# A two-direction state-space layer with its feed-forward part: B·C and the state update placed between the two parts of the outputs in twelve chunk pairs

## The chip, the core and the metric

The kernel runs on one core of a Trainium2 chip. The core has TensorE (matmuls, PE; its weight loads are listed apart as PEld), VectorE (DVE), ScalarE (ACT), GpSimd (POOL) and SyncE (SP), which here only issues DMAs. Each engine works through its own instructions in their order and waits on semaphores for the others. Matmuls write to PSUM, eight banks that TensorE, VectorE and ScalarE share; everything else lies in SBUF. The metric is the device time of one execution in microseconds (us); less is better.

## What is computed

Eight sequences of 512 tokens with 256 features pass through a layer norm, a state-space block (Mamba-2) once forward and once on the reversed sequence, a projection of both results with a residual, a second layer norm, and a feed-forward part with a low-rank correction, again with a residual. All of it is in 32-bit floats. The reference of one direction, cut:

```python
zxbcdt = x @ Win
z, xBC, dt = jnp.split(zxbcdt, [D_INNER, D_INNER + CONV_CH], axis=-1)
xBC = _silu(conv(xBC, convw) + convb)            # 4 taps along the sequence
xs, Bm, Cm = jnp.split(xBC, [D_INNER, D_INNER + NGROUPS * D_STATE], axis=-1)
dt = softplus(dt + dtb)
dA = exp(dt * -exp(Alog))
h = dA_t * h + dt_t * B_t * x_t                  # per head, 64 states, step by step
y_t = C_t . h
y = (y + D * xs) * silu(z)
y = y * rsqrt(mean(y * y) + 1e-05) * normw
return y @ Wout
```

There are 512 inner channels in 8 heads of 64, and 64 states.

## The kernel before

**Tiling.** A sequence is cut into four chunks of 128 tokens. A *pair* (b, c) is chunk c of the forward direction of sequence b together with chunk 3-c of the backward one; the 32 pairs are worked off in order (b, c). Within a chunk the recurrence is written as matrix products: the outputs of a pair are the sum of what the state at the chunk's start gives (h with C, scaled by the decay) and what the chunk's own tokens give (x times dt, with a 128x128 matrix per head, `lam`, which holds decays times B·C).

**The main loop** (`for i in range(n)`, L964) handles in iteration i the pair p = i and prepares the pair q = i+1, and mixes in pieces of other work: blocks of the input projection and convolution of the next sequences (`Block.project`, `tap`, `convolve`, `silu`; the blocks of an iteration are called `work[0]` to `work[3]`), gate projections (`Gates.project`, tile pz), and the tails of finished chunks (`Tail`: output projection pm, second norm, feed-forward pf, store). The order of instructions on each engine is the order in which the loop writes them; `pin()` (L60) fixes it at the end of each iteration. No scheduler moves anything.

**The steps of a pair on TensorE, by line.** `outputs` (L637): the state's part, from h and dec, for chunks 1 to 3 (32 matmul instructions; each 32-bit matmul is two instructions, a transpose one), and then the part within the chunk, from xdt and lam (32); both add into the two tiles py (L643). `add_state` (L657): pst (L663), the chunk's contribution to the state. `turn` (L584): transposes of q's x, tiles pxs (L588). `work[0].project`: pp (L419). `Tail.turn`: pxt (L784). `norm_sum`: ss (L702). A gate: pz (L499). `cb` (L603): B·C of q (L609), from which `mix` (L614) makes q's lam. Then pf (L791), pm (L751), and the other blocks and gates.

**The steps on the other engines.** VectorE: `evict` (L675) adds py into yg; `new_state` (L665) adds pst to the decayed state in chunks 1 and 2 (in chunk 0 it is a copy, on ScalarE); `scan` (L570) and `mix` make lam; `convolve` (L432) takes three instructions per block; the tail's `residual` (L758) and `add_ffn` (L794) read pm and pf. ScalarE: `tap` (L430), copies of the turned tiles (L590, L786), silus, squares (L691), the sums for the norm (L709), `skip` (L623). GpSimd: `times_gate` (L684), `scale_x` (L599), `scale_c` (L566), `decay_state` (L633), and small norm arithmetic. In each odd sequence, chunks 1 and 2 also hold the series that turns the raw step sizes of the next two sequences into dt and decays (`Steps`, L326, on ScalarE and VectorE).

**PSUM.** One bank holds a constant; the other seven are pools, in each of which tiles take turns: p_proj with 3 banks (pp, pz, pst), p_tr with 2 (pxs, pxt, ss, cb and other turned tiles), p_y with 2 (py, pf, pm). A tile waits until the last reader of the tile that had its bank before is done. The pools are set up as follows:

```python
p_proj = ctx.enter_context(tc.tile_pool(name="p_proj", bufs=3, space=PSUM))
p_tr = ctx.enter_context(tc.tile_pool(name="p_tr", bufs=2, space=PSUM))
p_y = ctx.enter_context(tc.tile_pool(name="p_y", bufs=2, space=PSUM))
```

Of the kernel before, what the change touches and what calls it, by code (L numbers as in the profile page):

```python
# [14 lines left out]
P = 128  # L15
NB, L, DM = 8, 512, 256
NC = L // P
DI = 512
NS = 64
NH, HD = 8, 64  # L20
NK = DM // P
NBLK = DI // P
# [9 lines left out]
def tile_bimamba_ffn(  # L32
# [39 lines left out]
    pe, dve, act, pool, sp = nc.tensor, nc.vector, nc.scalar, nc.gpsimd, nc.sync  # L72
# [4 lines left out]
# [3 lines that stand above are left out]
# [8 lines left out]
    def ps(p, shape, name):  # L88
        return p.tile(shape, F32, name=name, tag=p.name)
# [32 lines left out]
    for d in range(2):  # L122
# [4 lines left out]
        rows = slice(d * 64, (d + 1) * 64)  # L127
# [150 lines left out]
    def softplus_v(b0, of):  # L278
        v, e = sm("v", b0) if b0 == 0 else of, sm("e", b0)
        act.activation(v, of, AF.Identity, bias=dtb_col[:, 0:1])  # L280
        act.activation(e, v, AF.Abs)
        act.activation(e, e, AF.Exp, scale=-1.0)
        return v, e

    def steps_raw(b0):

        half = L // 2
        pd = ps(p_tr, [P, half], f"pdt_{b0}")
        quarters = [(i, j) for i in range(NSG) for j in range(2)]
        for k in range(NK):  # L290
            for n, (i, j) in enumerate(quarters):
                pe.matmul(
                    pd[32 * n:32 * (n + 1), :], lhsT=wd2[:, k, :],
                    rhs=seq[b0 + i]["xhT"][:, k, j * half:(j + 1) * half],
                    start=(k == 0), stop=(k == NK - 1), skip_group_check=True, tile_position=(0, 32 * n),
                )
        raw = convp.tile([P, half], F32, name=f"raw_{b0}", tag="raw", bufs=1)
        act.copy(raw, pd)
        return b0, raw
# [82 lines left out]
    def steps_last(b0):  # L382
        g = seq[b0]["g"]
        last = g["last"] = sm("last", b0, (P, 64))
        act.activation(last[F], fold[F], AF.Copy, scale=upto[F, P:])
        act.activation(last[W], fold[W], AF.Copy, scale=onward[W, 0:1])

    def steps_by_token(b0):
        g = seq[b0]["g"]
        dt, wl = g.pop("rows")  # L390
        pt = ps(p_tr, [P, 2, P], f"pdw_{b0}")
        pe.transpose(pt[:, 0, :], dt, ident)
        pe.transpose(pt[:, 1, :], wl, ident)
        g["dw"] = sm("dw", b0, (P, 2, P), bufs=2)
        act.copy(g["dw"], pt)
# [128 lines left out]
    class Pair:  # L524
# [58 lines left out]

        def turn(m, d, pool_of=None):  # L584

            pt = ps(pool_of or p_tr, [P, DI], f"pxs_{m.name}_{d}")
            for blk in range(NBLK):
                pe.transpose(pt[:, blk * P:(blk + 1) * P], m.s["xc", d][:, blk, m.tcol[d]], ident)  # L588
            m.xw[d] = m.tile("xs", (P, DI), 4, d)
            act.copy(m.xw[d], pt)  # L590
# [43 lines left out]
                    hb(m.h_new), hb(m.s["h"]), tot.unsqueeze(2).to_broadcast([P, NH, HD]), ALU.mult  # L634
                )

        def outputs(m):  # L637

            m.py = [ps(p_y, [P, NBLK, P], f"py_{m.name}_{d}") for d in range(2)]

            def add(d, h, lhsT, rhs, first, last):
                blk, two = divmod(h, 2)
                pe.matmul(  # L643
                    m.py[d][two * HD:(two + 1) * HD, blk, :], lhsT=lhsT, rhs=rhs, start=first, stop=last,
                    skip_group_check=True,
                )

            order = [(d, 2 * blk + two) for blk in range(NBLK) for d in range(2) for two in range(2)]
            if m.c:
                for d, h in order:  # L650
                    rows = slice(d * NS, (d + 1) * NS)
                    add(d, h, m.s["h"][rows, h * HD:(h + 1) * HD], m.dec[rows, h, :], h < 2, False)
            for d in range(2):
                for h in range(NH):
                    add(d, h, m.xdt[d][:, h * HD:(h + 1) * HD], m.lam[d][:, h, :], m.c == 0 and h < 2, h >= NH - 2)

        def add_state(m):  # L657
            if m.c == NC - 1:
# [36 lines left out]
        def squares(m):  # L695
            return m.s["gates", m.c // 2].sz[:, :, :, m.c % 2, :]

        def norm_sum(m):

            m.ss = ps(p_proj if (m.b, m.c) == (NB - 1, 1) else p_tr, [P, 2, P], f"ss_{m.name}")  # L700
            for d in range(1 if m.folded else 2):
                pe.transpose(m.ss[:, d, :], m.squares()[:, d, 0, :], ident)  # L702

# [21 lines left out]
    class Tail:  # L725
# [51 lines left out]
        def bias2(t):  # L777
            t.adds.tensor_tensor(t.x1[:, 0, :], t.x1[:, 0, :], bf_sb, ALU.add)

        def turn(t):  # L780
            at = begin[ends.index((t.b, t.c))]
            pt = ps(p_proj if at == n - 3 else p_tr, [P, NK, P], f"pxt_{t.name}")
            for k in range(NK):
                pe.transpose(pt[:, k, :], t.xh[:, k * P:(k + 1) * P], ident)  # L784
            t.xT = outp.tile([P, NK, P], F32, name=f"xT_{t.name}", tag="xT")
            act.copy(t.xT, pt)  # L786
# [14 lines left out]
    first = {key: Block(0, *key) for key in blocks}  # L801
# [9 lines left out]
    for half, (mv, rs) in enumerate(halves):  # L811
        for j in range(2):
            c = 2 * half + j
            dve.tensor_scalar(xh[:, c, :], xh[:, c, :], mv[:, j, 0:1], rs[:, j:j + 1], ALU.subtract, ALU.mult)
    seq[0]["xhT"] = seqp.tile([P, NK, L], F32, name="xhT_0", tag="xhT", bufs=3)
    pt = [ps(p_tr, [P, L], f"pxh_0_{k}") for k in range(NK)]
# [14 lines left out]
    def conv(*key):  # L831
        first[key].convolve()
# [27 lines left out]
    st = Steps(0, *softplus_v(0, pdt))  # L860
# [12 lines left out]
    order = [(b, c) for b in range(NB) for c in range(NC)]  # L873
    n = len(order)
# [4 lines left out]
    q = pairs[0]  # L879
# [13 lines left out]
    gates.project_one(0, 0)  # L893
    gates.project_one(1, 0)
    steps_by_token(0)
    q.turn(0)
    conv(1, 2)
    q.scale_x(0)
    first[1, NBLK].silu()
# [34 lines left out]
    ends = [(b, c) for b in range(NB) for c in (1, 2, 0, 3)]  # L934

    begin = [min(j + NC - 1, n - 1 + (j % NC) // 2) if j >= n - NC else j + NC - 1 for j in range(n)]
    tails = {}

    def when(t, *what):
        for one in t if isinstance(t, list) else [t]:  # L940
            if one is not None:
                for w in what:
                    if w:
                        getattr(one, w)()

    def begun(at):
        return [tails[j] for j in range(n) if begin[j] == at]

    def gated(i):
# [10 lines left out]
            ones += [(g.project, g.silu, d, half) for half in range(2)]  # L960
        return ones

    st = raw = late = before = None
    for i in range(n):  # L964
        p, q = pairs[i], pairs.get(i + 1)
        b, c = order[i]
        t, t0 = begun(i), begun(i - 1)
        gates = None

        def gate(j):  # L970
            nonlocal gates
            if gates is None:
                gates = gated(i)
            if j < len(gates):
                gates[j][0](*gates[j][2:])

        def gate_silu(j):
            if j < len(gates):
                gates[j][1](*gates[j][2:])
# [3 lines left out]
        even = b % NSG == 0  # L983
# [10 lines left out]
        hold = q is not None and c == NC - 1  # L994
        if work[0] is None or hold:
            when(t0, "norm2")
        if b:
            p.decay_state()
            if q:
                q.scale_c()  # L1000
        p.outputs()

        soon = b and c < 2
        if soon:
# [4 lines left out]
        early = q is not None and b == NB - 1  # L1009
        if early:  # L1010
            q.scan(0)
        for d in range(2):
            p.evict(d)
            p.times_gate(d)
        p.add_state()
        p.new_state()
        if q:
            q.turn(0)
            if not hold:
                q.turn(1)  # L1020
        if hold:
            when(before, "norm_sum", "norm_mean")
            when(late, "silu")
        elif work[0] is not None:
            when(t0, "norm2")
# [4 lines left out]
        if hold:  # L1030
            if work[0] is None:
                gate(0)
            q.turn(1)
        if not q:
            when(t[:1], "bias1", "project")
        when(t0, "turn")
        if not hold:
            when(before, "norm_sum", "norm_mean")
        if not p.folded:
            for d in range(2):  # L1040
                p.square(d)
# [6 lines left out]
        if q:  # L1048
            if not hold or work[0] is not None:
                gate(0)  # L1050
            q.cb()
            gate_silu(0)
            if i == 0:
                steps_last(0)
            if p.folded:
                for d in range(2):
                    p.square(d)
            for d in range(2):
                q.scale_x(d)
# [50 lines left out]
        if raw is not None and c == 1:  # L1110
            st = Steps(b + 1, *softplus_v(b + 1, raw))
# [29 lines left out]
            q.decay_state()  # L1141
        when(work[2], "convolve")
        when(work[3], "convolve_aside")
        if st and not even and c == 2:
            steps_by_token(ahead)
            st = None
        late, before = work[2:] if i else work[1:], p
# [7 lines left out]
        if even and c == 3 and ahead < NB:  # L1155
            raw = steps_raw(ahead)
# [2 lines left out]


    t, t0 = begun(n), begun(n - 1)
    when(before, "norm_sum", "norm_mean")
    when(t0[:1], "scales", "norm2")
    when(t, "bias1")
    when(before, "norm_power")
    when(t0[:1], "bias2")
    when(t0[1:], "scales", "norm2")
    when(t, "project")
    when(t0, "turn")
    when(t[0], "residual")  # L1170
    when(t0[1:], "bias2")
    t[1].residual((0,))
# [3 lines left out]
    when(t0[:1], "add_ffn", "store")  # L1176
    when(t[1], "norm2_v")
    when(t0[1:], "add_ffn", "store")
    when(t, "bias2", "turn")
    for one in t:  # L1180
        when(one, "ffn", "add_ffn", "store")
    pin()
# [40 lines left out]
```

## Time and profile before

| what | value |
|---|---|
| median of three executions | 612.42 us (611.91 to 612.53) |
| the profiled execution | 612.31 us, span of its instructions 610.5 us |
| granted TensorE clock | 0.998 of full speed |
| VectorE busy in 180:220, 300:340, 340:380 (us of 40) | 39.09, 38.97, 38.01 |
| TensorE busy in the same | 40.00, 39.86, 40.00 |
| pp matmuls (L419) | 151.1 us, 320 instructions |
| pm (L751), pz (L499) | 115.8 us and 106.5 us |
| py (L643) | 63.0 us, 1024 instructions |
| py's weight loads | 55.3 us |

The profile is of one execution. A group's line gives engine, line, operation, tiles written and read, the sizes, the count and the times; of a matmul the part of the array in use stands first (128*128 is all of it, 64*64 a quarter). The ends of matmuls are modelled, so that the start of one group to the start of the next tells more than a duration. The chain of waits follows the work that ended last back in time; its shares tell which engine set the end where.

### The profile page before, as it was taken

What the parts mean: (1) busy time and instruction counts of PE and PEld (TensorE: products, weight loads), DVE (VectorE), ACT (ScalarE), POOL (GpSimd) and SP (SyncE); (2) the same over time, 40 slices, a digit from 0 to 9 for tenths busy, and PEclk for the clock granted to TensorE, in tenths of its full rate; (3) what the DMA queues carried; (4) which work ended last, traced back from release to release, by engine and by line L of the source; (5) the groups of instructions that cost most, each with busy time, mean ns of one, the idle gap of its engine ahead of it and who ended that gap; (6) DMA issues with size and microseconds to landing.
All of it is one profiled execution on the core that took longest, in us unless ns stands there. A gap on an engine that the chain in (4) does not pass through costs nothing.

```text
span 610.5 us, 11975 instructions
## 1 busy us (share of the span) xinstructions
PE 591.1 (97%) x4296; PEld 424.6 (70%) x4296; DVE 543.2 (89%) x818; ACT 437.9 (72%) x988; POOL 471.1 (77%) x580
## 2 busy tenths in 40 slices
PE   5989989999999999999999999999999999999997
PEld 2467757667776687766767677767767767777875
DVE  5888988889999989988999998988999998897964
ACT  3788796777877687885887877786978856755541
POOL 3287885787858898878859799678976889599983
PEclk9999999999999999999999999999999999999999
DMA  7476342123065323135025422443006442444011
GB/s 220 139 245 190 113 112 77 29 74 103 4 200 155 122 87 110 54 84 157 19 90 186 124 77 88 122 123 119 24 5 195 121 122 88 122 121 122 18 53 36
DMA packets 36252, 64.82 MB, mean 106 GB/s; under 512 B 8608, under 2 KB 23392, under 8 KB 36192
## 3 DMA queue, kind: packets, MB, share of 16 engines
q1 hardware_dynamic: 34048, 64.00, 34.7%
q8 instruction: 34, 0.56, 0.4%
q10 hardware_dynamic: 2144, 0.04, 0.2%
q14 instruction: 26, 0.21, 0.1%
HBM read 59.12 MB, written 4.72 MB: 105 GB/s over the span
## 4 chain that ended last, share of the span: by engine, by line
PE 67%; DVE 15%; ACT 10%; POOL 4%; issue 2%; DMA 1%; SPq 0%; DVEq 0%; ACTq 0%; POOLq 0%
PE pp L419 16%; PE pm L751 14%; PE pz L499 12%; PE py L643 10%; PE pf L791 4%; PE pxs L588 4%; DVE lam L577 4%; DVE xc L437 3%; PE pst L663 3%; PE cb L609 1%; DVE lam L615 1%; ACT yg L623 1%; ACT sz L691 1%; DVE yg L677 1%; ACT xc L455 1%
## 5 line engine op out<-in xcount | busy, mean ns | idle before, releaser
L437 DVE SCALAR_TENSOR_TENSOR xc<-pp,conv_sb,xc 128x511 f32<-128x511 f32 x180 | 133.4, 744 | 24.1 <-ACT xc L430 19.9
L419 PE MATMUL pp<-xhT,win_sb 128*128 128x512 f32 x320 | 151.1, 598 | 1.0 <-ACT v L280 0.5
L577 DVE TENSOR_TENSOR_SCAN lam<-lam,seed 128x512 f32<-128x512 f32 x128 | 145.7, 1198 | 0.5 <-DMA lam<-dat 0.5
L684 POOL TENSOR_TENSOR yg<-yg,sz 128x512 f32<-128x512 f32 x64 | 81.1, 1289 | 62.8 <-DVE yg L677 58.2
L751 PE MATMUL pm<-wy,yg 128*128 128x256 f32 x512 | 115.8, 379 | 0.0
L499 PE MATMUL pz<-xhT,win_sb 128*128 128x256 f32 x448 | 106.5, 380 | 0.3 <-ACT sz L522 0.3
L751 PEld LDWEIGHTS pm<-wy,yg 128*128 128x128 f32 x512 | 97.0, 190 | 13.4 <-issue 0.3
L499 PEld LDWEIGHTS pz<-xhT,win_sb 128*128 128x128 f32 x448 | 82.4, 190 | 17.7 <-issue 5.3
L419 PEld LDWEIGHTS pp<-xhT,win_sb 128*128 128x128 f32 x320 | 57.8, 192 | 46.8 <-issue 42.0
L623 ACT ACTIVATE yg<-xc,dcol 128x128 f32<-128x128 f32 x256 | 81.3, 393 | 0.5
L615 DVE TENSOR_TENSOR lam<-lam,cb 128x1024 f32<-128x1024 f32 x64 | 74.9, 1211 | 0.5 <-PE cb L609 0.5
L430 ACT ACTIVATE xc<-pp,conv_sb 128x512 f32<-128x512 f32 x64 | 49.7, 779 | 32.2 <-PE pp L419 32.1
L599 POOL TENSOR_TENSOR xdt<-xs,dw 128x512 f32<-128x512 f32 x64 | 66.5, 1045 | 1.1 <-ACT xs L590 1.1
L643 PE MATMUL py<-lam,xdt 128*64 128x128 f32 x1024 | 63.0, 276 | 0.6 <-POOL xs L599 0.6
L643 PEld LDWEIGHTS py<-lam,xdt 128*64 128x64 f32 x1024 | 55.3, 137 | 8.8 <-issue 3.6
L590 ACT COPY xs<-pxs 128x512 f32<-128x512 f32 x64 | 35.1, 588 | 32.9 <-PE pxs L588 32.8
L507 ACT ACTIVATE sz<-pz 128x512 f32<-128x512 f32 x56 | 33.2, 592 | 31.0 <-PE pz L499 30.9
L599 POOL TENSOR_TENSOR xs<-xs,dw 128x512 f32<-128x512 f32 x48 | 50.2, 1045 | 3.8
L691 ACT ACTIVATE sz<-yg 64x512 f32<-64x512 f32 x80 | 50.1, 626 | 0.7
L677 DVE TENSOR_TENSOR yg<-py,yg 128x512 f32<-128x512 f32 x64 | 41.6, 682 | 8.1 <-ACT yg L623 5.4
L588 PEld LDWEIGHTS pxs<-ident,xc 128*128 128x128 f32 x256 | 28.1, 141 | 27.4 <-issue 13.4
L720 POOL TENSOR_TENSOR sz<-sz 128x512 f32<-128x512 f32 x32 | 41.0, 1281 | 0.5 <-ACT sz L693 0.3
(237 smaller groups left out, 956.6 us busy)
## 6 DMA issues: line engine op xcount, KB each, us to landing
lam<-dat SPq DMA_DIRECT2D x64, 512.0 KB
x<-in_x_dram SPq DMA_DIRECT2D x36, 128.0 KB
out_dram<-x SPq DMA_DIRECT2D x32, 128.0 KB
x<-in_x_dram SPq DMA_DIRECT2D x7, 512.0 KB
win_sb<-in_win_dram SPq DMA_DIRECT2D x2, 640.0 KB
win_sb<-in_win_dram SPq DMA_DIRECT2D x2, 512.0 KB
wot<-in_wout_t_dram SPq DMA_DIRECT2D x2, 512.0 KB
v<-raw SPq DMA_DIRECT2D x48, 4.0 KB
```

Of the source, the lines that this page charges most:

```text
L419: pe.matmul(pp, lhsT=win_sb[:, d, k, c0:c0 + P], rhs=s["xhT"][:, k, :], start=(k == 0), stop=(k == NK - 1),)
L437: dve.scalar_tensor_tensor(self.acc[:, to], self.pp[:, of], self.w[:, 3 - j:4 - j], self.acc[:, to], ALU.mult, ALU.add,)
L499: pe.matmul(pz[:, j, :], lhsT=win_sb[:, d, k, blk * P:(blk + 1) * P], rhs=self.s["xhT"][:, k, cols], start=(k == 0), stop=(k == NK - 1),)
L577: dve.tensor_tensor_scan(lam, lam, sd, 0.0, ALU.mult, ALU.add)
L588: pe.transpose(pt[:, blk * P:(blk + 1) * P], m.s["xc", d][:, blk, m.tcol[d]], ident)
L599: pool.tensor_tensor(hb(to), hb(m.xw[d]), dw[:, j, cols].unsqueeze(2).to_broadcast([P, NH, HD]), ALU.mult)
L615: dve.tensor_tensor(m.lam[d], m.lam[d], m.pcb[d].unsqueeze(1).to_broadcast([P, NH, P]), ALU.mult)
L623: act.activation(yg[:, blk, :], m.s["xc", d][:, blk, m.tcol[d]], AF.Copy, scale=dcol[:, d, blk:blk + 1])
L643: pe.matmul(m.py[d][two * HD:(two + 1) * HD, blk, :], lhsT=lhsT, rhs=rhs, start=first, stop=last, skip_group_check=True,)
L684: pool.tensor_tensor(yg, yg, m.gates(d), ALU.mult)
L691: act.activation(m.squares()[d * 64:(d + 1) * 64, j], yg[j * 64:(j + 1) * 64], AF.Square)
L751: pe.matmul(t.pm[d], lhsT=yg[:, blk, :], rhs=wy[:, d, blk, :], start=(blk == 0), stop=(blk == NBLK - 1),)
```

## The change

It concerns the pairs of sequences 1 to 6 with chunk 0 or 1 (`follows`, twelve pairs, called *near*). In them:

- `outputs` is split in two, `outputs_of_state` and `outputs_within`. Between them now stand `q.cb()` and `p.add_state()`; cb leaves its place behind the gate.
- `new_state` comes before the evictions and gate products, not after them. In chunk 1 this moves one VectorE instruction ahead of two others; in chunk 0 it is ScalarE's copy, whose place among ScalarE's instructions stays the same.
- q's turned tiles (pxs) are taken from p_proj instead of p_tr.
- The two brief tiles pxt and ss are taken from p_y, the banks of the outputs, instead of p_tr.

In all other pairs the order and the pools stay. Only the raw step sizes' tile (`steps_raw`, three times) goes from p_tr to p_proj for good; other edits to default pools leave the tiles where they were. The diff, cut:

```diff
     def steps_raw(b0):
...
-        pd = ps(p_tr, [P, half], f"pdt_{b0}")
+        pd = ps(p_proj, [P, half], f"pdt_{b0}")
...
-        def outputs(m):
+        def add(m, d, h, lhsT, rhs, first, last):
+            blk, two = divmod(h, 2)
+            pe.matmul(
+                m.py[d][two * HD:(two + 1) * HD, blk, :], lhsT=lhsT, rhs=rhs, start=first, stop=last,
+                skip_group_check=True,
+            )
+
+        def outputs_of_state(m):
 
             m.py = [ps(p_y, [P, NBLK, P], f"py_{m.name}_{d}") for d in range(2)]
...
+            if m.c:
+                for blk in range(NBLK):
+                    for d in range(2):
+                        for h in (2 * blk, 2 * blk + 1):
+                            rows = slice(d * NS, (d + 1) * NS)
+                            m.add(d, h, m.s["h"][rows, h * HD:(h + 1) * HD], m.dec[rows, h, :], h < 2, False)
+
+        def outputs_within(m, d):
+            for h in range(NH):
+                m.add(
+                    d, h, m.xdt[d][:, h * HD:(h + 1) * HD], m.lam[d][:, h, :], m.c == 0 and h < 2, h >= NH - 2
                 )
...
+    def follows(i):
+
+        return NC <= i < n - NC - 1 and order[i][1] < 2
+
...
-        p.outputs()
+        p.outputs_of_state()
+        series = st is not None and not even and c == 2
+        near = follows(i) and not series
+
+        brief = p_y if near else p_proj if i == n - 2 else p_tr
+        turns = p_proj if near else p_tr
+        if near:
+            q.cb()
+            p.add_state()
+        for d in range(2):
+            p.outputs_within(d)
...
+        if near:
+            p.new_state()
         for d in range(2):
             p.evict(d)
             p.times_gate(d)
-        p.add_state()
-        p.new_state()
+        if not near:
+            p.add_state()
+            p.new_state()
         if q:
-            q.turn(0)
+            q.turn(0, turns)
             if not hold:
-                q.turn(1)
+                q.turn(1, turns)
...
-        when(t0, "turn")
-        if not hold:
-            when(before, "norm_sum", "norm_mean")
+
+        for one in t0:
+            one.turn(brief)
+        if not hold and before:
+            before.norm_sum(brief)
+            before.norm_mean()
...
-            q.cb()
+            if not near:
+                q.cb()
```

More of the change, by code (lines that the diff above doesn't have):

```diff
@@ L584, in turn @@
         def turn(m, d, pool_of=None):
-            pt = ps(pool_of or p_tr, [P, DI], f"pxs_{m.name}_{d}")
+            pt = ps(pool_of or p_proj, [P, DI], f"pxs_{m.name}_{d}")
             for blk in range(NBLK):
@@ L635, in decay_state @@
                 )
-        def outputs(m):
-            m.py = [ps(p_y, [P, NBLK, P], f"py_{m.name}_{d}") for d in range(2)]
[L641 to L645, printed above, removed]
-                )
[L648 to L655, printed above, removed]
+        def add(m, d, h, lhsT, rhs, first, last):
[5 more added lines that the diff above has]
+        def outputs_of_state(m):
+            m.py = [ps(p_y, [P, NBLK, P], f"py_{m.name}_{d}") for d in range(2)]
+            if m.c:
[8 more added lines that the diff above has]
+                    d, h, m.xdt[d][:, h * HD:(h + 1) * HD], m.lam[d][:, h, :], m.c == 0 and h < 2, h >= NH - 2
+                )
         def add_state(m):
@@ L696, in squares, with norm_sum @@
             return m.s["gates", m.c // 2].sz[:, :, :, m.c % 2, :]
-        def norm_sum(m):
-            m.ss = ps(p_proj if (m.b, m.c) == (NB - 1, 1) else p_tr, [P, 2, P], f"ss_{m.name}")
+        def norm_sum(m, pool_of=None):
+            m.ss = ps(pool_of or p_y, [P, 2, P], f"ss_{m.name}")
             for d in range(1 if m.folded else 2):
@@ L778, in bias2, with turn @@
             t.adds.tensor_tensor(t.x1[:, 0, :], t.x1[:, 0, :], bf_sb, ALU.add)
-        def turn(t):
-            at = begin[ends.index((t.b, t.c))]
-            pt = ps(p_proj if at == n - 3 else p_tr, [P, NK, P], f"pxt_{t.name}")
+        def turn(t, pool_of=None):
+            pt = ps(pool_of or p_y, [P, NK, P], f"pxt_{t.name}")
             for k in range(NK):
@@ L895, in tile_bimamba_ffn @@
     steps_by_token(0)
-    q.turn(0)
+    q.turn(0, p_tr)
     conv(1, 2)
@@ L1014, in tile_bimamba_ffn @@
             p.times_gate(d)
-        p.add_state()
-        p.new_state()
+        if not near:
+            p.add_state()
+            p.new_state()
         if q:
-            q.turn(0)
+            q.turn(0, turns)
             if not hold:
-                q.turn(1)
+                q.turn(1, turns)
         if hold:
-            when(before, "norm_sum", "norm_mean")
+            before.norm_sum(brief)
+            before.norm_mean()
             when(late, "silu")
@@ L1032, in tile_bimamba_ffn @@
                 gate(0)
-            q.turn(1)
+            q.turn(1, turns)
         if not q:
             when(t[:1], "bias1", "project")
-        when(t0, "turn")
-        if not hold:
-            when(before, "norm_sum", "norm_mean")
+        for one in t0:
+            one.turn(brief)
+        if not hold and before:
+            before.norm_sum(brief)
+            before.norm_mean()
         if not p.folded:
@@ L1143, in tile_bimamba_ffn @@
         when(work[3], "convolve_aside")
-        if st and not even and c == 2:
+        if series:
             steps_by_token(ahead)
@@ L1161, in tile_bimamba_ffn @@
     t, t0 = begun(n), begun(n - 1)
-    when(before, "norm_sum", "norm_mean")
+    before.norm_sum(p_tr)
+    before.norm_mean()
     when(t0[:1], "scales", "norm2")
@@ L1168, in tile_bimamba_ffn @@
     when(t, "project")
-    when(t0, "turn")
+    for one in t0:
+        one.turn(p_tr)
     when(t[0], "residual")
@@ L1178, in tile_bimamba_ffn @@
     when(t0[1:], "add_ffn", "store")
-    when(t, "bias2", "turn")
+    when(t, "bias2")
+    for one in t:
+        one.turn(p_tr)
     for one in t:
```

## The prediction, made before the changed kernel ran

> **What bounds the kernel now.** I read the busy shares first, then the shares of the chain of waits, then TensorE's timeline through one of the pairs that the change touches, then the chain in order of time.
>
> ```profile
> PE 591.1 (97%) x4296; PEld 424.6 (70%) x4296; DVE 543.2 (89%) x818; ACT 437.9 (72%) x988; POOL 471.1 (77%) x580
> PE 67%; DVE 15%; ACT 10%; POOL 4%; issue 2%; DMA 1%; SPq 0%; DVEq 0%; ACTq 0%; POOLq 0%
> ```
>
> TensorE is busy nearly all the time and holds two thirds of the chain; VectorE (89%) is close behind. A change in TensorE's order can therefore pay only by making TensorE's own stream shorter, and only in stretches where TensorE is the chain. The stream through pair (4,1) (sequence 4, chunk 1), matmuls only; the sizes such as 64*64 are the part of the array in use, rows*columns:
>
> ```profile
> 349.20 1.88 PE L419 MATMUL pp<-xhT,win_sb 128*128 128x512 f32 x4
> 351.01 1.10 PE L643 MATMUL py<-dec__3540,h__3587 64*64 64x128 f32 x32
> 352.05 1.97 PE L643 MATMUL py<-lam,xdt 128*64 128x128 f32 x32
> 353.84 1.03 PE L663 MATMUL pst<-xs,bn 128*64 128x512 f32 x4
> 354.80 1.09 PE L588 MATMUL pxs<-ident,xc 128*128 128x128 f32 x8
> 355.73 1.88 PE L419 MATMUL pp<-xhT,win_sb 128*128 128x512 f32 x4
> ...
> 357.78 1.89 PE L499 MATMUL pz<-xhT,win_sb 128*128 128x256 f32 x8
> 359.60 0.45 PE L609 MATMUL cb<-cc,bb 64*64 64x128 f32 x8
> 359.98 1.13 PE L791 MATMUL pf<-wf,xT 128*128 128x256 f32 x4
> 360.95 3.62 PE L751 MATMUL pm<-wy,yg 128*128 128x256 f32 x16
> ```
>
> Ends are modelled, so read start to start. There is no idle gap, yet time is lost: cb sits alone, 64*64, between two groups at 128*128.
>
> **The price of a change of array shape.** pz before cb lasts 359.60-357.78 = 1.82 us; the pz at 364.40, followed by a 128*128 group at 366.13, lasts 1.73: +0.09. Inside the state's part of py four matmuls pass every 0.109 us, so its 32 need 0.87 and take 1.03: 0.16 lost at entrance and exit. By that rate cb's eight need 0.22 and take 0.38: +0.16. pm's sixteen take 3.45, so pf's four need 0.86 and take 0.97: +0.10. cb in its old place thus costs 0.22 of work and 0.36 of changing shape.
>
> Two pages of the Trainium skill disagree here. "TensorE: Matmul & The Clock Gate" (Step-by-step) says the next weights are loaded while the running matmul still streams; taken alone, that prices the three borders at 0 and the whole move at 0. "TensorEngine Tiling (Array Packing)" (Key Properties) says a change of tiling mode drains the array, without a price. The rows decide: 0.36 us per cb.
>
> **The change, part by part.** Twelve pairs: sequences 1 to 6, chunks 0 and 1.
>
> - Chunk 1: cb follows the state's part, both 64*64, and adds 0.22 there; the old place gives back 0.58 (0.09+0.38+0.10). Net -0.36. pst moves ahead of the rest of py, both 128*64, so no border is added.
> - Chunk 0 has no state's part; cb stands between pp (128*128) and pst (128*64) and still pays its whole 0.38. Net -0.20.
>
> On paper: 6 x 0.36 + 6 x 0.20 = 3.4 us.
>
> *New waits in the near pairs.* I set each wait of the changed order against the time at which the old trace has its releaser done (times from the first py). In chunk 1 the pst, turns and pp now use the three p_proj banks. pst waits for a silu that ended 1.0 us before the pair; the second turn (due at +4.5) waits for a convolution done at +3.2 to +3.9; pp (due at +4.9) waits for the state's h, which VectorE now adds before both evictions: +3.9 to +4.6, instead of +5.0 to +5.7 in the old order, where it would have been late. The evictions come 0.6 later but end together as before; GpSimd's gate product behind them has 1.6 us idle at 498 and is busy with dec in even sequences: nothing. The two brief tiles, now in py's banks, wait for evictions that end at about +4.5 and +5.1 (0.6 later in even sequences), due at +6.6 and +6.8: nothing. In chunk 0 one wait shows: the second turn (due at +3.6) waits for ScalarE's copy of h,
>
> ```profile
> 336.51 0.59 ACT L670 COPY h__3587<-pst 128x512 f32<-128x512 f32 x1
> ```
>
> which stands behind two silus in ScalarE's queue and ends at +3.7 in (2,0) and (4,0): a wait of 0.14 each, with pp queued behind. steps_raw's tile in p_proj: its releaser is 1.9 us early. ScalarE's, GpSimd's and SP's orders are the same instruction by instruction, so no DMA is passed.
>
> **What of the 3.4 reaches the end.** The chain leaves TensorE once per odd sequence:
>
> ```profile
> 284.71 1.73 PE pp L419 x4
> 286.47 0.34 ACT xc L430
> ...
> 295.46 0.32 ACT e L282
> 295.81 0.31 DVE pzu L339
> ...
> 317.62 0.64 ACT xc L455
> 318.31 0.33 PE pxs L588
> ```
>
> From the end of pp in (3,1) it runs 32 us over ScalarE and VectorE (the step sizes' series) and meets TensorE again in (3,3). The same stands at 143-175 and 430-462. What TensorE saves after that pp is waited away at the meeting; what it does before it counts. cb now stands before that pp: +0.22. So:
>
> - up to the first meeting: (1,0) -0.20, (1,1) +0.22: 0.0.
> - second and third: (2,0) -0.06 and (2,1) -0.36, but VectorE, dense from 295 to 368, ends its residual only 0.42 before TensorE needs the bank in (2,2), so of the 0.42 about 0.36 passes; (3,0) -0.20; (3,1) +0.22: -0.34 each.
> - after the third: (6,0) -0.20. In (6,1) VectorE is dense from a convolution that waited for ScalarE, fed by TensorE ahead of the pair, to the residual that (6,2) waits for:
>
> ```profile
> 495.43 2.32 DVE L437 SCALAR_TENSOR_TENSOR xc<-pp,conv_sb,xc 128x511 f32<-128x511 f32 x3 [1.05 <-ACT xc L430]
> ...
> 508.72 0.99 DVE L758 SCALAR_TENSOR_TENSOR x<-pm,rms,x 128x256 f32<-128x256 f32 x2
> ```
>
> It ends 0.17 before its bank is written, so of (6,1)'s 0.36 only 0.11 passes: -0.31 in all.
>
> Sum: 0.0 - 0.34 - 0.34 - 0.31 = **-1.0 us**. The profiled execution took 612.31 (span 610.5 and 1.8 around it), 0.1 under the median of 612.42: **611.3 us**.
>
> Unknown costs: whether cb runs on after the state's part without a border, which no row shows. At worst it pays its full 0.16 as in chunk 0, and half of the gain is gone (0.16 in (2,1), (3,1), (4,1), (5,1): +0.6, so 611.9). At best the hidden waits at banks are shorter than counted: -0.3. I take no border, as the state's part shows none between its own two directions.
>
> **Rivals.**
>
> 1. *The whole saving arrives.* For it: TensorE's 97%. Against it: the three 32 us stretches in which the chain is not TensorE's. Price: 612.3 - 3.4 + 0.3 of waits = 609.2; half of it, if VectorE's dense stretches slide with TensorE, 610.5. Chance 0.20.
> 2. *Nothing to see.* The +0.22 before the series is paid and the gains ahead of it are waited away at VectorE, whose 38.0 to 39.1 us of 40 in the odd stretches speak for that; against it, VectorE has idle time of 0.9 and 2.0 us at 386 and 405, where it waits for ScalarE. Price: 3 x 0.22 - 0.2 in (6,0): 612.8. Chance 0.16.
> 3. *Slower: p_proj's three banks.* In near pairs two turns more pass through them, so pst, turns and pp now wait for VectorE's convolution, h and a copy. In this trace the margins are 0.3 to 1.3 us, the smallest about 0.35. If that turnover comes one VectorE instruction (0.75) late in each near pair, TensorE loses 0.75-0.35 = 0.4 in each: 12 x 0.4 - 1.0 = +3.8, 616.1. It decides once the lateness is above 0.35 + 1.0/12 = 0.43, and shows by 0.2% from 0.53. For it: VectorE is dense from 295 to 368. Against it: h goes first now, and the convolutions' times are those of the old trace. Chance 0.10.
>
> The forecast itself, 610.8 to 611.9, has 0.54. A measurement here tells 0.2% (1.2 us) from no change, so the line is 611.2, close to the forecast: of the 0.54 about 0.18 falls under it. Faster: 0.18+0.20 = 0.38. Slower: 0.10, and 0.02 of rival 2. Same: the remaining 0.50. The range 609.9 to 612.9 takes in the forecast with both ends of the unknown border, rival 2, and the part of rival 1 that lies near half.
>
> **What would show it.** In the profile after: pz to pf in near pairs 1.73 and 0.86 long with no cb between; py, cb in 1.25 us in chunk 1 (1.41 if there is a border); pst, py and pxs following without idle; a wait of TensorE at the second turn in (2,0) and (4,0), ended by the copy of h; the pp of (3,1) about 0.3 earlier than before relative to the meeting ahead of it; TensorE waiting about 0.6 longer in (3,2) and (3,3). Waits of pxs or pp for VectorE in most near pairs would show rival 3; an end near 609 that the series slid along, rival 1.

## The result, and the profile after

| | before | after |
|---|---|---|
| median, runs side by side | 612.47 us (611.91 to 613.26, 4 runs) | 619.31 us (618.95 to 620.09, 4 runs) |
| profiled execution | 612.31 us, span 610.5 us | 619.58 us, span 617.7 us |
| granted TensorE clock | 0.998 | 1.0 |

The ratio is 1.0112, with a 95% interval of 1.0095 to 1.013: the change costs 6.8 us, where 1.0 us less was forecast. The page after, its busy shares, its chain by engine, and the rows of the gate projection and of GpSimd's gate product:

```profile
PE 592.3 (96%) x4296; PEld 427.9 (69%) x4296; DVE 551.4 (89%) x818; ACT 437.7 (71%) x988; POOL 469.8 (76%) x580
...
PE 67%; DVE 16%; ACT 10%; POOL 4%; issue 2%; DMA 0%; SPq 0%; DVEq 0%; ACTq 0%; POOLq 0%
...
L687 POOL TENSOR_TENSOR yg<-yg,sz 128x512 f32<-128x512 f32 x64 | 80.7, 1281 | 72.0 <-DVE yg L680 72.0
...
L499 PE MATMUL pz<-xhT,win_sb 128*128 128x256 f32 x448 | 106.8, 381 | 6.2 <-DVE dt L351 5.4
```

VectorE has the same 818 instructions as before and is busy 8.2 us longer (551.4 against 543.2): some of them got slower. And pz now waits 5.4 us for the line that ends the series of the step sizes (`dt`, L351); in the page before, pz's whole idle time was 0.3 us.

To place the loss, I took the start of the first py of each pair in the trace after, less its start in the trace before, less the 0.83 us by which sequence 0 already ran later, where the two kernels have the same instructions:

| up to pair | (1,2) | (1,3) | (2,3) | (3,2) | (3,3) | (4,3) | (5,2) | (5,3) | (6,3) | (7,3) |
|---|---|---|---|---|---|---|---|---|---|---|
| us later | -0.55 | +2.19 | +2.17 | +1.61 | +4.34 | +4.32 | +3.76 | +6.49 | +6.30 | +6.3 |

(First pairs are left out: there the changed order itself puts cb and pst ahead of py.) Everything is lost in three steps of 2.73 us, from (odd,2) to (odd,3): in the stretches of the series. The matmuls, shown in the timeline of TensorE through pair (4,1) after, did what they were meant to:

```profile
356.16 1.10 PE L639 MATMUL py<-dec__3540,h__3589 64*64 64x128 f32 x32
357.08 0.40 PE L609 MATMUL cb<-cc,bb 64*64 64x128 f32 x8
357.41 1.08 PE L666 MATMUL pst<-xs,bn 128*64 128x512 f32 x4
...
361.10 1.88 PE L419 MATMUL pp<-xhT,win_sb 128*128 128x512 f32 x4
...
363.14 1.89 PE L499 MATMUL pz<-xhT,win_sb 128*128 128x256 f32 x8
364.87 1.03 PE L793 MATMUL pf<-wf,xT 128*128 128x256 f32 x4
365.74 2.54 PE L754 MATMUL pm<-wy,yg 128*128 128x256 f32 x11
```

Start to start, py and cb take 1.25 us together, pz 1.73 and pf 0.87: no border is paid at cb any more. Now the chain in order of time in the stretch of sequence 3, from pp in (3,1) to where it meets TensorE again:

```profile
287.73 1.73 PE pp L419 x4
...
298.48 0.32 ACT e L282
298.83 0.31 DVE pzu L339
299.15 0.97 DVE r L340
300.15 1.13 DVE e L341
301.30 2.36 DVE pzu L342
...
323.48 0.33 PE pxs L588
```

It is the chain of before with two long pieces in it, L341 and L342, both products of 128x128. Beside GpSimd's instructions, in the timeline of all engines of the kernel after:

```profile
298.32 0.18 DVE L228 BATCH_NORM_AGGREGATE ln_mv<-ln_st 128x2 f32<-128x6 f32 x1
298.83 0.29 DVE L339 TENSOR_SCALAR pzu<-e 128x128 f32<-128x128 f32 x1 [0.32 <-ACT e L282]
...
300.08 1.04 POOL L633 TENSOR_TENSOR h__3161<-h__2979,tot 128x512 f32<-128x512 f32 x1
...
300.15 1.12 DVE L341 TENSOR_TENSOR e<-e,r 128x128 f32<-128x128 f32 x1
...
301.08 2.42 POOL L566 TENSOR_TENSOR dec__3025<-dec__3025,cc 128x1024 f32<-128x1024 f32 x1
301.30 2.35 DVE L342 TENSOR_TENSOR pzu<-e 128x128 f32<-128x128 f32 x1
...
305.62 0.30 DVE L349 SCALAR_TENSOR_TENSOR pzu<-r,e 128x128 f32<-128x128 f32 x1
```

and the same place in the kernel before:

```profile
295.53 0.18 DVE L228 BATCH_NORM_AGGREGATE ln_mv<-ln_st 128x2 f32<-128x6 f32 x1
295.81 0.29 DVE L339 TENSOR_SCALAR pzu<-e 128x128 f32<-128x128 f32 x1
...
297.13 0.29 DVE L341 TENSOR_TENSOR e<-e,r 128x128 f32<-128x128 f32 x1
297.20 1.12 POOL L633 TENSOR_TENSOR h__3161<-h__2979,tot 128x512 f32<-128x512 f32 x1
297.45 1.02 DVE L342 TENSOR_TENSOR pzu<-e 128x128 f32<-128x128 f32 x1
...
298.28 2.41 POOL L566 TENSOR_TENSOR dec__3016<-dec__3016,cc 128x1024 f32<-128x1024 f32 x1
...
300.44 0.41 DVE L349 SCALAR_TENSOR_TENSOR pzu<-r,e 128x128 f32<-128x128 f32 x1
```

Read who starts first. Before, L341 starts 0.07 us ahead of GpSimd's decay of the state (L633) and takes 0.29; L342 starts behind L633 and ends at 298.47, 0.15 after L633's end (298.32). After, L633 is the first by 0.07, and L341 ends 0.15 after L633's end (301.27, 301.12); by then L566 has started, and L342 ends 0.15 after *its* end (303.65, 303.50). L349 of before does the same behind L566 (300.85, 300.69). The three are those of the series with both inputs in SBUF. L346 and L348, which read their one input, or one of their two, from PSUM, ran beside L566 in their usual 0.29. The series took 5.80 us (from L339 to the eviction) before and takes 7.96 after, in each odd sequence. The three lines make 6.2 of VectorE's 8.2 us; most of the rest is in additions behind the start of the last pair, where only 0.1 us more is lost.

Why did the order flip? GpSimd gets to L633 by four small norm products that wait for VectorE's `ln_mv` (L228); the series waits for ScalarE's e. From the end of `ln_mv` to L339 it was 0.10 us before and is 0.33 after: e comes 0.23 later, the 0.22 of cb ahead of pp. (That it is cb is tried below.) In TensorE's timeline after, most of the loss surfaces as one wait:

```profile
304.53 0.27 PE L705 MATMUL ss<-ident,sz 128*128 128x128 f32 x1
306.60 1.99 PE L499 MATMUL pz<-xhT,win_sb 128*128 128x256 f32 x8 [1.80 <-DVE dt L351]
```

pz's bank is the one in which the series works.

### The profile page after: what moved, and what is told of

It reads as the page before. It is cut to its first block, busy times and chain, and to the rows that moved or that the text cites. A ratio compares the mean times of both kernels' runs of the same rounds, so it can differ in the third digit from the quotient of the medians.

```text
span 617.7 us, 11955 instructions
## 1 busy us (share of the span) xinstructions
PE 592.3 (96%) x4296; PEld 427.9 (69%) x4296; DVE 551.4 (89%) x818; ACT 437.7 (71%) x988; POOL 469.8 (76%) x580
## 4 chain that ended last, share of the span: by engine, by line
PE 67%; DVE 16%; ACT 10%; POOL 4%; issue 2%; DMA 0%; SPq 0%; DVEq 0%; ACTq 0%; POOLq 0%
PE pp L419 16%; PE pm L754 14%; PE pz L499 12%; PE py L639 9%; PE pxs L588 4%; PE pf L793 4%; DVE lam L577 4%; DVE xc L437 3%; PE pst L666 3%; PE cb L609 1%; DVE lam L615 1%; ACT yg L623 1%; DVE pzu L342 1%; ACT sz L694 1%; ACT xc L430 1%
```

## The experiments

**Theory A**: the new order sends the series 0.22 us later, GpSimd's product then starts first, and VectorE's products of two SBUF operands stand still for the length of GpSimd's. **Theory B** is rival 3, the turnover of p_proj's banks in all near pairs. **Theory C**: the state update ahead of the evictions delays GpSimd's gate products, whose wait for the eviction grew from 58.2 to 72.0 us. Ratios are to the kernel before, run beside.

### Which pairs cost

```diff
-        return NC <= i < n - NC - 1 and order[i][1] < 2
+        return NC <= i < n - NC - 1 and order[i] and order[i][1] < 2 and not (order[i][0] % 2 and order[i][1] == 1)
```

> The new order in the first pair of every inner sequence and in the second pair of the even ones only; the second pair of the odd sequences, after which the series of the step sizes starts, keeps the old order. Theory A (the new order sends the series 0.22 us later, GpSimd's two products then start ahead of VectorE's two products of two SBUF operands, and these stand still, 2.2 us three times): none of the three losses, the start as before, so about 611.4 (1.1 under before's 612.5). Theory B (the banks of the projections turn over late in all the changed pairs): 9 of 12 changed pairs left, at least 617. Theory C (the state update ahead of the evictions delays the gate's products): 9 of 12 left, about 617.

Measured: 612.62 us, ratio 0.9990 (0.9984 to 0.9997). And the complement, the new order in only those three pairs:

```diff
-        return NC <= i < n - NC - 1 and order[i][1] < 2
+        return NC <= i < n - NC - 1 and order[i][0] % 2 and order[i][1] == 1
```

> The new order in the second pair of the odd sequences 1, 3 and 5 only. Theory A: the three losses in full, 3 x (0.22 + 2.16) = 7.1 over before, about 619.6, with VectorE's two products e<-e,r and pzu<-e at 1.1 and 2.35 us in all three. Theories B and C: 3 of 12 changed pairs, so a quarter of the 6.8, about 614.2.

Measured: 620.30 us, ratio 1.0117 (1.0102 to 1.0132), 7.3 us; L341 and L342 take 1.13 and 2.35 in all three stretches. Three pairs cost all of it and nine cost nothing, so B and C fall as causes; so does the new pool of `steps_raw`, which the kernel with the nine pairs keeps. The nine brought 0.4 us by the medians (0.6 by the ratio) where 1.1 was expected; that is taken up below.

### The flip without the change, and the change without the flip

The kernel before, with one instruction of ScalarE twice, so that only the series comes later:

```diff
         act.activation(e, v, AF.Abs)
+        if b0:
+            act.activation(e, v, AF.Abs)
```

> The kernel before, with the absolute value of the step sizes taken twice on ScalarE in sequences 1, 3 and 5, some 0.3 us ahead of the series; nothing else changed. Theory A: the series starts 0.3 us later against GpSimd's products, which start by another instruction, and loses the same race: 3 x (2.16 + 0.3) = 7.4 over before, about 619.9. Theories B and C: nothing of the change is in it, so at most 3 x 0.3, 613.4.

Measured: 620.17 us, ratio 1.0115 (1.0100 to 1.0130). Its timeline (the lines are two further down in this kernel):

```profile
300.62 1.04 POOL L635 TENSOR_TENSOR h__3163<-h__2980,tot 128x512 f32<-128x512 f32 x1
...
300.88 0.93 DVE L343 TENSOR_TENSOR e<-e,r 128x128 f32<-128x128 f32 x1
...
301.84 2.35 DVE L344 TENSOR_TENSOR pzu<-e 128x128 f32<-128x128 f32 x1
```

An instruction of 0.31 us in the old order loses as much as the whole change. L343 waited less than in the kernel after (0.93 against 1.12) because it started 0.26 behind GpSimd and not 0.07; its end is fixed by GpSimd's. The other way round, the changed kernel with 0.21 us more work on GpSimd, ahead of L633:

```diff
+        if not even and c == 2 and b < NB - 1:
+            idle = small.tile([P, 1], F32, name=f"idle_{b}", tag="idle")
+            pool.tensor_scalar(idle, neghalf[:, 0:1], -1.0, None, ALU.mult)
         if b:
             p.decay_state()
```

> The changed kernel, with one more small product (128x1) on GpSimd ahead of the decay of the state in the third pair of sequences 1, 3 and 5: work is only added. Theory A: GpSimd's 128x512 product starts some 0.1 us later, behind VectorE's e<-e,r instead of 0.07 us ahead of it; VectorE's two products take 0.29 and about 1.0 us again instead of 1.1 and 2.35, and the three losses go: ratio to before about 1.000 to 1.001. Theories B and C, or if it is not the order of the two starts: unchanged or slower, 1.011 to 1.012.

Measured: 612.68 us, ratio 1.000 (0.9991 to 1.0009). Its timeline:

```profile
297.26 0.21 POOL L1005 TENSOR_SCALAR idle<-neghalf 128x1 f32<-128x1 f32 x1
...
297.33 0.29 DVE L341 TENSOR_TENSOR e<-e,r 128x128 f32<-128x128 f32 x1
297.43 1.09 POOL L633 TENSOR_TENSOR h__3165<-h__2981,tot 128x512 f32<-128x512 f32 x1
297.65 1.02 DVE L342 TENSOR_TENSOR pzu<-e 128x128 f32<-128x128 f32 x1
```

L341 is first again, by 0.10, and 6.8 us are gone although work was only added. The other two stretches read alike (leads of 0.10 and 0.13). So the order of those two starts is the cause of the loss.

### Is it the operands?

The reciprocal and the product e go to the series' own bank of PSUM; a copy of the product stays in SBUF, so that no product has two SBUF inputs. One product is added.

```diff
-            pzu = ps(p_proj if m.b0 else p_tr, [P, 2, P], f"pzu_{m.b0}")
-            m.z, m.u = pzu[:, 0, :], pzu[:, 1, :]
+            pzu = ps(p_proj if m.b0 else p_tr, [P, 4, P], f"pzu_{m.b0}")
+            m.z, m.u, m.w, m.y = (pzu[:, j, :] for j in range(4))
...
-            dve.reciprocal(m.r, m.z)
-            dve.tensor_tensor(m.e, m.e, m.r, ALU.mult)
-            dve.tensor_tensor(m.u, m.e, m.e, ALU.mult)
+            dve.reciprocal(m.w, m.z)
+            dve.tensor_tensor(m.y, m.e, m.w, ALU.mult)
+            dve.tensor_tensor(m.e, m.e, m.w, ALU.mult)
+            dve.tensor_tensor(m.u, m.e, m.y, ALU.mult)
...
-            dve.scalar_tensor_tensor(m.z, pol, 1.0, m.e, ALU.add, ALU.mult)
+            dve.scalar_tensor_tensor(m.z, pol, 1.0, m.y, ALU.add, ALU.mult)
```

In the changed kernel:

> The changed kernel, with the reciprocal and its product of the series written to the bank of PSUM that the series has already, so that no product of it has two operands in SBUF (one product more, 0.29 us). Theory A: the two products take 0.29 us beside whatever GpSimd does; the 2.8 us that they lost in the changed kernel, less the added 0.29, are gone three times: about 619.3 - 7.5 to 612. Between that and 610.9 if the chain leaves the series. Theories B and C: no better than 619.3, by the added product up to 620.2.

Measured: 611.64 us, ratio 0.9978 (0.9970 to 0.9987). Its timeline:

```profile
297.00 1.04 POOL L634 TENSOR_TENSOR h__3164<-h__2981,tot 128x512 f32<-128x512 f32 x1
...
297.05 0.29 DVE L341 TENSOR_TENSOR pzu<-e,pzu 128x128 f32<-128x128 f32 x1
297.38 0.29 DVE L342 TENSOR_TENSOR e<-e,pzu 128x128 f32<-128x128 f32 x1
...
297.70 0.29 DVE L343 TENSOR_TENSOR pzu<-e,pzu 128x128 f32<-128x128 f32 x1
```

GpSimd is first, by 0.05, and no product of VectorE's waits for it. L342 here still writes to SBUF, and the L342 that waited before wrote to PSUM: the inputs decide, not where the result goes. In the kernel before:

> The kernel before with the series in PSUM as in the last experiment of this kind. Theory A: in the kernel before only pzu<-e stood still, 1.02 us instead of 0.29; 0.73 less 0.29 for the added product, so 0.44 three times off, 1.3 us: ratio 0.998. If the changed kernel's loss were in the series' length alone and not in the two products, nothing: 1.000 to 1.001.

Measured: 611.86 us, ratio 0.9978 (0.9970 to 0.9986), the 1.3 us expected: the kernel before already paid a part of this wait, in L342 and L349. The exact agreement is in part luck: in the trace, behind sequence 0, the first two series bring 0.4 us each and the third 0.05, because VectorE stands still for 0.43 us there ahead of L351, for a reason that the profile doesn't show.

### Which of the moved parts sends the series late

First with cb moved a little:

```diff
         if near:
-            q.cb()
+            if even or c != 1:
+                q.cb()
             p.add_state()
...
+        if near and not even and c == 1:
+            q.cb()
         for one in t0:
             one.turn(brief)
```

> The changed kernel, but in the second pair of the odd sequences B.C of the next pair is written behind the projection pp that the series waits for, and no longer ahead of it; the new order stays everywhere else. Theory A: the series starts as it did before the change, ahead of GpSimd's product, so the three losses of 2.2 us and the three 0.22 us go: ratio to before about 0.998 to 1.000. Theories B and C: all 12 pairs are still changed, as in the changed kernel 1.011.

A miss: 619.76 us, ratio 1.0115 (1.0099 to 1.0130). Two lines of its timeline say why:

```profile
291.78 0.60 ACT L507 ACTIVATE sz<-pz 128x512 f32<-128x512 f32 x1 [0.20 <-PE pz L499]
...
298.92 0.29 DVE L339 TENSOR_SCALAR pzu<-e 128x128 f32<-128x128 f32 x1 [0.48 <-ACT e L282]
```

ScalarE's queue to e also holds the silu of pz. With cb between them, pp to pz is 2.58 us, start to start, instead of 2.05; ScalarE waits 0.20 for pz, and e is again late. So "behind pp" wasn't enough. With cb behind pz, where it was, and all else of the new order kept:

```diff
         if near:
-            q.cb()
+            if even or c != 1:
+                q.cb()
             p.add_state()
...
-            if not near:
+            if not near or (not even and c == 1):
                 q.cb()
```

> The changed kernel, but in the second pair of the odd sequences B.C of the next pair is written at its old place, behind the projections pp and pz; the state's part, the state update and the brief tiles keep their new order there. Theory A: with nothing added ahead of pp and ahead of pz, on which ScalarE's way to the series depends, the series starts with GpSimd's product behind VectorE's e<-e,r, as before the change: that product 0.29 us again in all three, the losses gone, ratio to before 0.998 to 1.001. If the loss comes from the state update or the brief tiles of that pair: 1.011 as in the changed kernel.

Measured: 612.88 us, ratio 1.0002 (0.9994 to 1.0011); L341 takes 0.29 in all three. B·C's place in three pairs decides; the state update and the brief tiles there cost nothing that shows.

### Towards a better version

Three more kernels were tried; two of them change the second pairs of the even sequences, which give back what they save. In the trace after, VectorE's instructions from 196 to 214 stand 3.01 us later than before, and from the addition of the state on 3.22: standing first now, it waits for GpSimd's decay. The kernel after around (2,1):

```profile
213.41 1.04 POOL L633 TENSOR_TENSOR h__2205<-h__2059,tot 128x512 f32<-128x512 f32 x1
...
214.48 0.69 DVE L675 TENSOR_TENSOR h__2205<-h__2205,pst 128x512 f32<-128x512 f32 x1
215.09 1.28 DVE L680 TENSOR_TENSOR yg<-py,yg 128x512 f32<-128x512 f32 x2
```

TensorE gives the 0.36 back in the state's part of the next pair, (2,2):

```profile
226.21 1.48 PE L639 MATMUL py<-dec__2056,h__2205 64*64 64x128 f32 x32
227.62 1.97 PE L639 MATMUL py<-lam,xdt 128*64 128x128 f32 x32
```

It takes 1.41 us, start to start, instead of 1.04: the second tile of py waits for the residual, which reads the tile that had its bank, and starts 0.06 us after the residual's end.

One of the three kernels had the series in PSUM, cb behind pp as above, and the addition of the state behind both evictions in all second pairs:

```diff
-        if near:
+        if near and not (c == 1):
             p.new_state()
...
         if not near:
             p.add_state()
+        if not near or (c == 1):
             p.new_state()
```

> The changed kernel with the series in PSUM, B.C behind pp in the second pair of the odd sequences, and the state update behind the evictions again in the second pairs (so that VectorE does not wait there for GpSimd's decay of the state). Theory A: the borders' 0.36 us of the second pairs and 0.2 of the first arrive, some 1.7 us, and 1.3 us of the series: ratio 0.995, below the 0.9978 that the changed kernel with the series in PSUM had. If the give-back in the second pairs of the even sequences is not by the state update, about 0.997.

A miss: 614.35 us, ratio 1.0022 (1.0013 to 1.0032). TensorE's timeline in its pair (2,1):

```profile
213.14 1.09 PE L589 MATMUL pxs<-ident,xc 128*128 128x128 f32 x8
214.47 1.98 PE L420 MATMUL pp<-xhT,win_sb 128*128 128x512 f32 x4 [0.24 <-ACT xs L591]
```

With the addition moved back, pp gets the bank of a turned tile and waits for its copy: pxs to pp is 1.33 us instead of 0.93. That is rival 3's mechanism, in a variant. The next two have the series in PSUM and the old order in the odd sequences' second pairs; the second of them also puts the addition between the two evictions:

> The series in PSUM, and the new order in the first pairs and in the second pairs of the even sequences only. If the two savings add up (0.8 us that the trace without the odd sequences' second pairs is shorter, 1.2 us of the series in PSUM alone): 2.0 us, ratio 0.9967. If the chain takes one of them back: 0.998, like the series in PSUM alone.

Measured: 611.16 us, ratio 0.9974 (0.9966 to 0.9983), between the two expectations; the interval takes in both. For the second:

```diff
-        if near:
+        if near and c == 0:
             p.new_state()
         for d in range(2):
             p.evict(d)
             p.times_gate(d)
+            if near and c and d == 0:
+                p.new_state()
```

> The same kernel, and in the second pairs of the even sequences the addition of the state stands between the two evictions on VectorE, so that VectorE doesn't stand still 0.1 us for GpSimd's decay of the state; the 128x512 tile that waits for its bank loses at most what the eviction takes, 0.6 us, less what it had to spare. If the 0.1 us is what is given back there: 0.1 to 0.36 us less three times, ratio 0.9965 or less. If the bank decides: up to 0.3 us more three times, 0.998.

Measured: 611.10 us, ratio 0.9975 (0.9965 to 0.9985). The two can't be told apart: VectorE's wait is gone, but in (2,1) and (4,1) pp comes 0.29 us late, behind the addition (pxs to pp 1.22 us instead of 0.93). Both beat the kernel before; against the series in PSUM alone (0.9978) the intervals don't tell what the new order adds.

## Why the prediction was wrong

- **The price of a change of shape**: right. 0.36 us per second pair ((odd,1) to (odd,2) in the trace after: -0.36 each), 0.20 per first pair ((0,3) to (1,1): -0.19), and no border between the state's part and cb.
- **Waits in first pairs**: right. From (1,3) to (2,1) the trace after has -0.04, where -0.06 was forecast.
- **"cb now stands before that pp: +0.22."** The place and the 0.22 were right (0.23 measured at L339). The step that failed is the one behind it: the 32 us over ScalarE and VectorE were taken as a fixed length that slides with pp. GpSimd's products don't slide with pp, since they hang on `ln_mv`; a margin of 0.07 us turned over, and the series became 2.16 longer, three times: 6.5 of the 6.8 us. (The step of 2.73 is this 2.16, the 0.22, and the 0.36 of (odd,1) that is waited away at the meeting, as forecast.) The rows stood in the trace of before, L342 at 1.02 where L341 of the same size had 0.29, and I had listed GpSimd's part as "nothing" after looking at its gate product alone. The Trainium skill, "SBUF — State Buffer" (Who interferes with whom), says that a VectorE instruction with two SBUF inputs and a GpSimd instruction that reads SBUF exclude each other for the whole instruction, and that the issue order decides who blocks. These runs agree, to 0.15 us; I had not held it against this change.
- **(2,1), (4,1) and (6,1)**: mis-sized. Forecast: of 0.42 in (2,0) and (2,1) 0.36 passes, and of (6,1) 0.11. TensorE's 0.36 was given back each time in the next pair, net 0. In (2,2) and (4,2), 0.21 of it is VectorE's wait for the decay of the state, which "h first" brought and which I had not priced. The spare time at the residual was as forecast: in (2,2) the first matmul into the second tile of py starts 2.85 us later than before, which is VectorE's 3.22 less 0.36. But the state's part, once stopped, took longer to its end: it comes out at +3.00, so another 0.15 is lost (0.11 in (6,2)). Why is not shown.
- **The sum again**: with these at 0, -1.0 becomes -1.0 + 0.30 + 0.30 + 0.11 = -0.3 us. The changed kernel with the flip undone by GpSimd's extra product had 1.000; in its trace the last pair starts 0.15 us earlier than before, counted from sequence 0. With the 6.5 of the series, -0.3 makes +6.2; the trace after has +6.3 behind sequence 0, the medians +6.8. So apart from the series and those three pairs the working holds, and without the flip the change is worth nothing that can be measured.
- **Rivals**: 1 and 2 didn't come true. 3 gave the sign, by the wrong mechanism. None had an engine that is on no path of the forecast stopping one that is.

## What to carry to other kernels

When a step is moved, don't let a stretch of another engine slide as a block: look up what runs beside it on VectorE and GpSimd, which of VectorE's instructions have both inputs in SBUF, and by how much each is ahead. A short VectorE instruction that takes three times its usual length in one place is a sign that such a wait is there already. Putting one operand in PSUM took this kernel out of the race and cost one short instruction; it paid in both orders.

## What the runs showed of the hardware

A 128x128 product of VectorE with two SBUF inputs, 0.29 us alone, took up to 2.36 us beside a GpSimd product of 2.42 us and ended 0.15 us behind it. In all twelve stretches of the four kernels in which GpSimd was first (after, the three pairs alone, the later series, cb behind pp) both products waited, the second for the long one. In all twelve in which VectorE was first (before, the nine pairs, GpSimd's extra product, cb at its old place) the first took 0.29 us and the second waited only for the shorter GpSimd product, 1.02 us. A lead of 0.07 us decided. GpSimd lost far less: its 128x512 product took 1.12 us where VectorE was first by 0.07, and 1.04 where GpSimd was first or VectorE was first by 0.15. With one operand in PSUM the same product took 0.29 us beside the same GpSimd instruction.

The same wait seems to stand in the last sequence of the kernel before: VectorE's addition of the bias bf_sb to x (L778, both in SBUF) takes 0.39 us alone and 1.96 us beside L566. Its inputs were not moved to try it.

Not settled: in the first 45 us the profiled executions of all twelve other kernels fell 0.15 to 1.33 us behind that of before, also where the instructions are the same, and what a trace gains behind that point differs from the medians by up to 1.1 us (the kernel with cb at its old place: 0.8 less in the trace, 0.3 more in the median). The cause was not looked into; gains below 0.2% are not told apart here.
